# Query projections of five batches by Strassen's seven products, and the output projection begun one slot later

## The chip, the cores and the metric

The kernel runs on one core of one Trainium2 chip. The metric is the device time of one launch in microseconds (us); of several runs the median is given. A core has TensorE (PE, with its weight loads listed apart as PEld), VectorE (DVE), ScalarE (ACT), GpSimd (POOL) and SyncE (SP, which here only issues DMAs). Each engine works through its own list of instructions in the order in which the program wrote them and waits for semaphores of the others.

## The reference, cut to what matters

Cross-attention of 8 batches, 256 query tokens, 256 context tokens, width 1024, 32 heads of 32, all in fp32. The mask is all ones.

```python
x = (hidden - mu) * rsqrt(var + LN_EPS) * ln_gamma + ln_beta
Q = split_heads(x @ Wq.T)
scores = einsum('bhsd,bhtd->bhst', Q, K) * HEAD_DIM ** (-0.5)   # K, V: the context itself
probs = softmax(where(mask, scores, -inf))
attn = merge_heads(einsum('bhst,bhtd->bhsd', probs, V))
out = hidden + attn @ Wout.T
```

So each batch needs two products with a 1024 x 1024 matrix, 256 rows at a time: the query projection (Wq) and the output projection (Wout).

## The kernel before, in words

The program writes its own schedule. Its unit is a **slot** `n`, 0 to 63, of one group of four heads: `n = 8 * batch + group`. In slot `n` PE gets, in this order: the scores of group `n+1`; the product with V ("values") of group `n-2`; some steps of the output projection; one query tile (`make_q`, 8 matmuls of 256 columns, for a group six slots ahead); more steps of the output projection. Meanwhile the other engines run the softmax of group `n+1`. In the text, `i` is a slot's place in its batch, `n % 8`, and offsets are counted from the first scores matmul of the slot.

The softmax of a slot: DVE takes the mask and the maximum of eight 128x256 score tiles (L396), ACT takes their exponentials (L400) behind it, DVE the reciprocals of the sums (L407), POOL scales the eight tiles (L409, "normalize"), DVE transposes them in four 128x512 blocks (L415), ACT copies half of the blocks aside (L421), and SP issues the DMAs that bring the halves together (L472, L476), the loads of the slot between them.

Output projection (`product_steps`, L549). It is already made by Strassen's products: seven products `PRODUCTS` of four steps each, 28 steps for a batch, in the eight slots of the next batch. A step is one matmul of 512 columns whose weights are a block of the attention output `at` and whose moving operand is a block or a sum of blocks of Wout. The table `STEPS` says how many steps stand ahead of the query tile and how many behind the softmax's code in each slot. All accumulate in one PSUM bank, `po`, which has a single buffer: between certain products the bank is read out, by `keep` ("p1" on ACT, L559; "u2" and "u3" on DVE, L561) and `store` (DVE, L569, then a DMA by SP). Each read-out has to be done before PE's next step writes the bank. The sums of blocks of `at` are made by POOL (`sum_at`, L539): S1, S3, S2 at the end of slot `i = 1`, S4 in `i = 2`. Product S2 begins in slot `i = 2`, behind the query tile.

LayerNorm of later batches is spread over the slots: `bn_stats`, `bn_aggr` and `+eps` on DVE at the end of `i = 0` and `i = 1` (L211 to L216), and right behind them the power -1/2 on POOL (L217), which stands ahead of `sum_at` in POOL's list. The normalization is ACT's (L225, `i = 2, 3`), block transposes are DVE's (L290, `i = 3, 4`), and 16 small DMAs (`move_x`, L306) complete the transposed batch `xnT`.

`fold` multiplies Wq by gamma on POOL (L342) in slots 0 to 7 and copies the query bias to `qb` (L341). `sum_wo` (L177) makes the four Wout sums on POOL in slots 3 to 13.

The lines around the change, by their function in the listing: the query tile L319, its copy from PSUM to SBUF L327 to L333 on ACT, scores L362, values L492, copy of values to `at` L504.

## Time and profile before

| | us |
|---|---|
| median of 3 runs | 595.73 (595.67 to 596.32) |
| profiled execution, its own time | 596.43 |
| its span in the profile | 594.6 |
| PE busy | 582.0 |
| DVE / ACT / POOL busy | 458.3 / 407.0 / 347.5 |
| granted TensorE clock | 0.999 |

Times in the profile are counted from the span's start. `out<-in` are the program's names for tiles. A matmul of fp32 is kept as two records: the 56 query tiles of 8 matmuls with 256 columns are 896 records. In the list of groups a line ends with busy time, mean duration and the idle time ahead; in the timeline a line begins with start and length, merges equal neighbours, and ends with the idle time ahead of it and what ended it. A record's duration holds the pipeline's latency, so the cost of a matmul in a row of matmuls is the distance of starts, not the duration.

Slots are seen in the timeline by the first scores matmul: slot 33 (`i = 1` of a batch) begins at 305.70, slot 34 at 314.08, slot 35 at 323.35. In the steady part they last alternately 8.39 and 9.25 us, 70.56 for eight.

### The profile page before, as it was taken

How to read it: one execution, taken by the hardware profiler on the slowest of the kernel's cores; microseconds unless marked ns; L12 is line 12 of the kernel's file. 1: busy time of each engine (PE TensorE's matmuls, PEld its weight loads, DVE VectorE, ACT ScalarE, POOL GpSimd, SP SyncE). 2: the span in 40 equal slices, each digit the busy share in tenths (PEclk: the TensorE clock that was granted, in tenths of full speed). 3: DMA queues.
4: the chain of work that ended last, by engine and by line, in shares of the span. 5: the costliest groups of instructions: out<-in, count | busy, mean ns of one | idle time of the engine just before them, and what ended most of it. 6: DMA issues, size and time to landing. Idle time of an engine off the chain costs nothing.

```text
span 594.6 us, 18914 instructions
## 1 busy us (share of the span) xinstructions
PE 582.0 (98%) x6680; PEld 389.3 (65%) x6680; DVE 458.3 (77%) x1675; ACT 407.0 (68%) x1380; POOL 347.5 (58%) x630
## 2 busy tenths in 40 slices
PE   9999999999999999999999999999999999999997
PEld 8787776666666676666676667666666667654443
DVE  5878888697887878788787887878787677779801
ACT  4788786776777776686676876677677677667700
POOL 1568896987557644755447653484556564385600
PEclk9999999999999999999999999999999999999999
DMA  8566798545863667544674457654556355466541
GB/s 309 222 165 210 227 255 234 156 114 172 228 185 90 175 177 209 167 113 139 195 225 128 130 157 191 193 155 136 158 145 194 99 162 142 125 181 174 165 126 71
DMA packets 42063, 101.13 MB, mean 170 GB/s; under 512 B 8560, under 2 KB 8560, under 8 KB 41968
## 3 DMA queue, kind: packets, MB, share of 16 engines
q1 hardware_dynamic: 41680, 99.91, 57.4%
q8 instruction: 53, 0.87, 0.7%
q14 instruction: 42, 0.34, 0.2%
q10 hardware_dynamic: 288, 0.01, 0.0%
HBM read 51.65 MB, written 8.39 MB: 101 GB/s over the span
## 4 chain that ended last, share of the span: by engine, by line
PE 76%; POOL 12%; DVE 5%; issue 2%; DMA 2%; ACT 2%; SPq 1%; POOLq 0%; DVEq 0%; ACTq 0%
PE pq L319 29%; PE po_S L549 17%; PE sc L362 9%; PE pv L492 9%; POOL e L409 8%; PE po_A L549 7%; PE po L577 3%; DVE e L396 2%; POOL wo L177 2%; POOL wq L342 1%; PE busy L118 1%; DMA pT<-pc 1%; DVE pT L415 1%; DVE st L211 1%; DMA v<-in_kv_dram 1%
## 5 line engine op out<-in xcount | busy, mean ns | idle before, releaser
L409 POOL TENSOR_SCALAR e<-e,rden 128x256 f32<-128x256 f32 x512 | 237.3, 481 | 172.3 <-DVE rden L407 168.7
L400 ACT ACTIVATE e<-e,mn 128x256 f32<-128x256 f32 x512 | 254.3, 502 | 55.2 <-DVE mn L396 55.2
L319 PE MATMUL pq<-xnT,wq 128*128 128x256 f32 (+1 forms) x1008 | 230.7, 382 | 1.3 <-ACT q L327 1.2
L415 DVE STREAM_TRANSPOSE pT<-e 128x512 f32<-128x512 f32 x256 | 181.4, 709 | 55.4 <-POOL e L409 48.2
L319 PEld LDWEIGHTS pq<-xnT,wq 128*128 128x128 f32 x1008 | 188.9, 190 | 45.1 <-issue 17.9
L396 DVE CUSTOM_DVE_ANT_0 e<-sc,mb 128x256 f32<-128x256 f32 x512 | 185.4, 417 | 33.8 <-PE sc L362 33.5
L421 ACT COPY pc<-pT 128x512 f32<-128x512 f32 x128 | 79.2, 619 | 76.1 <-DVE pT L415 45.3
L549 PE MATMUL po_S<-wo,at 128*128 128x512 f32 x224 | 107.0, 603 | 3.3 <-DVE u L561 1.3
L400 ACT ACTIVATION_READ_ACCUMULATOR e<-e,mn 128x1 f32 x512 | 98.4, 192 | 0.0
L492 PE MATMUL pv<-pT,v 64*32 64x128 f32 x4096 | 74.6, 274 | 2.2 <-DMA pT<-pc 1.4
L362 PEld LDWEIGHTS sc<-k,q 32*128 32x128 f32 x1024 | 46.4, 184 | 46.3 <-issue 23.4
L362 PE MATMUL sc<-k,q 32*128 32x256 f32 x1024 | 74.3, 401 | 0.1
L492 PEld LDWEIGHTS pv<-pT,v 64*32 64x32 f32 x4096 | 57.3, 105 | 25.0 <-issue 12.9
L549 PEld LDWEIGHTS po_S<-wo,at 128*128 128x128 f32 x224 | 40.6, 189 | 38.8 <-issue 31.8
L549 PE MATMUL po_A<-wo,at 128*128 128x512 f32 x112 | 52.0, 598 | 0.0
L407 DVE RECIPROCAL rden<-den 128x2 f32<-128x2 f32 x256 | 39.3, 153 | 9.0 <-ACT e L400 6.3
L396 DVE DVE_READ_ACCUMULATOR2_ANT mn<- 128x1 f32 x512 | 42.7, 83 | 0.0
L549 PEld LDWEIGHTS po_A<-wo,at 128*128 128x128 f32 x112 | 20.8, 190 | 19.1 <-issue 18.4
L217 POOL TENSOR_TENSOR rstd<-ve,mhalf 128x1 f32<-128x1 f32 x16 | 9.4, 585 | 38.8 <-DVE ve L216 38.2
L504 ACT COPY at<-pv 128x128 f32<-128x128 f32 x128 | 26.1, 253 | 8.1 <-PE pv L492 8.1
L333 ACT ACTIVATE q<-pq,qb 128x256 f32<-128x256 f32 x48 | 22.6, 470 | 10.2 <-PE pq L319 10.2
L549 PE MATMUL po_S<-wo,s 128*128 128x512 f32 x56 | 26.9, 605 | 0.6 <-DVE r L569 0.6
(52 smaller groups left out, 299.7 us busy)
## 6 DMA issues: line engine op xcount, KB each, us to landing
v<-in_kv_dram SPq DMA_DIRECT2D x32, 512.0 KB, 4.3
pT<-pT SPq DMA_DIRECT2D x128, 128.0 KB, 2.3
pT<-pc SPq DMA_DIRECT2D x128, 128.0 KB, 3.9
k<-in_kv_dram SPq DMA_DIRECT2D x32, 256.0 KB, 3.4
x<-in_x_dram SPq DMA_DIRECT2D x14, 512.0 KB, 5.6
r<-in_x_dram SPq DMA_DIRECT2D x28, 256.0 KB, 4.4
out_dram<-r SPq DMA_DIRECT2D x28, 256.0 KB, 3.1
xnT<-xe SPq DMA_DIRECT2D x96, 64.0 KB, 3.1
```

Of the source, the lines that this page charges most:

```text
L319: nc.tensor.matmul(pqs[n], wq[:, o, c, :], xnTs[b](c), start=(c == 0), stop=(c == NC - 1),)
L333: nc.scalar.activation(q[:, :S].rearrange("p (s a k) -> p a s k", s=NS, a=NA), pqs.pop(n).rearrange("p (a s k) -> p a s k", s=NS, a=NA), A ...
L362: nc.tensor.matmul(scs[n][j][:, s, :], qs[n][r, ts(s, P)], ks[n - n % 2][r, n % 2, :], start=True, stop=True,)
L396: nc.vector.tensor_tensor_reduce(out=e[:, s, :], in0=pss[j][:, s, :], in1=mbs[n // NQ], scale=1.0, scalar=NO_SCORE, op0=ALU.add, op1=ALU.m ...
L400: nc.scalar.activation(e[:, s, :], e[:, s, :], AF.Exp, bias=mn[:, s : s + 1], scale=-1.0, accum_out=den[:, s : s + 1],)
L407: nc.vector.reciprocal(rden, dens[j])
L409: nc.gpsimd.tensor_scalar(es[j][:, s, :], es[j][:, s, :], rden[:, s : s + 1], 1.0, ALU.mult, ALU.mult,)
L415: nc.vector.transpose(pT[:, :, :, j, :, :].rearrange("p a i s k -> p (a i) s k"), es[j].rearrange("p s (b t) -> p b s t", t=K),)
L421: nc.scalar.copy(pc[:, :, ts(j, 2)], pT[:, 1, :, ts(j, 2)])
L492: nc.tensor.matmul(pvs[n][r][j * HD : (j + 1) * HD], vs[n - n % 2][ts(r, 2 * K), i, ds(n % 2 * P + j * HD, HD)], pT[ts(r, 2 * K), :, i, j, ...
L504: nc.scalar.copy(ats[b][:, c, :, ts(r, 2), :], pv.rearrange("p a s k -> p s a k"))
L549: nc.tensor.matmul(pos[b], operand(b, name)[:, c], wo[:, which, c], start=begins and c == 0, stop=c == NK - 1, skip_group_check=not begins,)
```

## The change

Queries of batches 3 to 7 are no longer made tile by tile, but as seven products of a Strassen scheme, one product in each slot of `i = 2, 3, 4, 5, 6, 7, 0`, none in `i = 1`. A product is 16 matmuls of 128 columns (`query_product`); its weights are 4 x 4 blocks of Wq or of sums of them, its moving operand is a quarter of `xnT` or a sum of quarters. Products accumulate in the `pq` bank; after each one `copy_product` reads it: four ACT activations for products 0, 1, 2, 5 and one DVE addition for 3, 4, 6. These copies stand behind the third transposed block in the softmax's code. The query of a batch lies in one tile `qa` with no second buffer, and its last column holds the bias, so that `qb` goes.

The sums of weights are made once on POOL (`sum_wq`, 16 additions of 128x512, in slots 9 to 20), the sums of quarters of `xnT` for each batch (`sum_x`, four additions: two in `i = 0`, one each in `i = 2` and `i = 3`). Three of the weight matrices, T1, B11 and T3, are written to DRAM once and come back through one tile `ring` of 1 MB, in two DMAs of 512 KB each, issued in `i = 0`, `i = 2` and `i = 4` of each batch, for the products of `i = 2`, `4` and `6`.

The output projection of batches 0 to 5 begins in `i = 1` in place of `i = 0`, has three places in a slot (behind the scores, behind the values, behind the softmax's code) and ends in `i = 0` of the batch after. Its first four steps stand in `i = 1` between scores and values, and `keep` "p1" is written right behind them, ahead of the softmax's code. Batch 6 keeps its former steps (`ENDS`). Query tiles of batches 0 to 2 go on as before, but slot 8 makes two and slot 9 none; the second of slot 8 uses the `po` bank.

Smaller parts: the mask is loaded batch by batch, 6 + 6 + 4 in place of 4 + 4 + 4 + 4 block moves in a slot, `at` in halves with three buffers, fewer buffers in `asp` and `sm`.

```diff
-    asp = ctx.enter_context(tc.tile_pool(name="asp", bufs=3))
+    asp = ctx.enter_context(tc.tile_pool(name="asp", bufs=2))
...
+    ring = const.tile([P, NK, NK, P], F32, tag="ring", name="ring")
+    sums_x = const.tile([P, 2, NK, NA, K], F32, tag="sx", name="sx")
+    kept = {
+        name: dram.tile([P, NK, NK * P], F32, tag=name, name=f"kept_{name}")
+        for name in ("T1", "B11", "T3")
+    }
...
     def fold(o):
 
-        nc.gpsimd.tensor_copy(qb[:, o : o + 1], qs[o][:, S:])
         nc.gpsimd.tensor_tensor(
-            wq[:, o], wq[:, o], gam.unsqueeze(2).to_broadcast([P, NC, P]), ALU.mult
+            wq[:, o], wq[:, o], gs.unsqueeze(2).to_broadcast([P, NC, P]), ALU.mult
         )
...
+    Q_PRODUCTS = (
+        ("S1", "ring", True), ("S4", "B22", False), ("A11", "ring", True), ("S2", "T2", False),
+        ("S3", "ring", False), ("A22", "T4", False), ("A12", "B21", True),
+    )
...
+    def query_product(b, p):
+        name, which, begins = Q_PRODUCTS[p]
+        if begins:
+            pqs[b] = ps_q.tile([P, NK, P], F32, tag="pq", name=f"pq_{b}_{name}")
+        x_ = x_part(b, name)
+        for o in range(NK):
+            w = weights(which, o)
+            for c in range(NK):
+                nc.tensor.matmul(
+                    pqs[b][:, o, :], w[:, c], x_[:, c], start=begins and o + c == 0,
+                    stop=c == NK - 1, skip_group_check=True,
+                )
...
-    STEPS = [((0, 4), (0, 3), (1, 3), (1, 2), (2, 2), (2, 1), (3, 1), (0, 3))] * (B - 2)
-    STEPS.append(((0, 4),) * 7 + ((0, 0),))
+    STEPS = ((0, 0, 0), (4, 0, 3), (0, 1, 2), (0, 2, 2), (0, 2, 1), (0, 1, 2), (0, 0, 3), (0, 1, 2),
+             (0, 2, 0))
+    ENDS = ((0, 0, 4),) * 7 + ((0, 0, 0),)
...
-    BATCH0 = (1, 2, 1, 1, 2, 1, 2, 1)
+    BATCH0 = (1, 2, 1, 1, 2, 1, 2, 1, 2, 0)
...
-                moves=tuple(first - 5 + i // 4 for i in range(16)),
+                moves=tuple(first - 5 + i // 6 for i in range(16)),
...
+    for n, which, *chunks in (
+        (9, "T1", 0, 1), (12, "T1", 2), (13, "T1", 3), (14, "T3", 0, 1), (15, "T3", 2, 3),
+        (16, "T2", 0, 1), (18, "T2", 2, 3), (19, "T4", 0, 1), (20, "T4", 2, 3),
+    ):
+        sums[n] += [partial(sum_wq, which, o) for o in chunks]
+    for n, b in firsts.items():
+        for slot, name in ((n - 2, "S1"), (n - 2, "S2"), (n, "S4"), (n + 1, "S3")):
+            sums[slot].append(partial(sum_x, b, name))
...
+    for n, b in firsts.items():
+        for slot, name in ((n - 2, "T1"), (n, "B11"), (n + 2, "T3")):
+            if b > SPLIT or name != "T1":
+                streams[slot] += [partial(load_ring, name, half) for half in range(2)]
...
         if n + 1 < N:
             scores(n + 1)
+        project_steps(n, 0)
+        hooks, now, behind = {}, [], []
+        for what, one, *args in evacuations[n]:
+            if what is keep and args == ["p1"] and one < B - 2:
+                keep(one, "p1")
+            elif one == B - 2:
+                now.append(partial(what, one, *args))
+            else:
+                hooks.setdefault(0 if i in (2, 3, 4, 6) else 1, []).append(partial(what, one, *args))
         if n >= 2:
             values(n - 2)
...
+        project_steps(n, 1)
+        copies = [partial(copy_q, q) for q in new_q[:1]]
         for q in new_q[:1]:
             make_q(q)
-
-        if b >= 0 and i == 1:
-            keep(b, "p1")
+        if n in products:
+            query_product(*products[n])
+            copies.append(partial(copy_product, *products[n]))
+        for one in now:
+            one()
...
-        if b >= 0:
-            product_steps(b, range(done, done + steps[i][1]))
-        for args in sums[n]:
-            sum_wo(*args)
+        project_steps(n, 2)
+        for one in sums[n]:
+            one()
         if b >= 0:
             for name in {1: ("S1", "S3", "S2"), 2: ("S4",)}.get(i, ()):
                 sum_at(b, name)
```

## The prediction

> **What bounds the kernel now.** First the page: busy times and the chain that ended last.

> ```profile
> PE 582.0 (98%) x6680; PEld 389.3 (65%) x6680; DVE 458.3 (77%) x1675; ACT 407.0 (68%) x1380; POOL 347.5 (58%) x630
> ...
> PE 76%; POOL 12%; DVE 5%; issue 2%; DMA 2%; ACT 2%; SPq 1%; POOLq 0%; DVEq 0%; ACTq 0%
> ```

> PE is the bound, and in the steady part it never waits: eight slots last 70.56 us, and that is the sum of their matmuls. POOL's 12% of the chain, listed in order of time, lies between 64 and 119 us (slots 5 to 12) and in the last five slots: early on POOL has no slack. What 128 columns cost is read from the timeline of PE: first the only query matmuls of that width (batch 0), then one slot with its query tile and three output steps.

> ```profile
> 12.52 2.05 PE L264 MATMUL pq<-xnT,wq 128*128 128x129 f32 x16
> 14.41 0.82 PE L319 MATMUL pq<-xnT,wq 128*128 128x257 f32 x3
> ...
> 305.70 1.15 PE L362 MATMUL sc<-k,q 32*128 32x256 f32 x16
> 306.77 1.16 PE L492 MATMUL pv<-pT,v 64*32 64x128 f32 x64
> 307.86 3.72 PE L319 MATMUL pq<-xnT,wq 128*128 128x256 f32 x16
> 311.42 2.74 PE L549 MATMUL po_A<-wo,at 128*128 128x512 f32 x6
> ```

> Starts count, not lengths: 16 records of 128 columns take 14.41 - 12.52 = 1.89, 16 of 256 take 311.42 - 307.86 = 3.56, 6 of 512 take 314.08 - 311.42 = 2.66. In each row one record costs 0.10 more (the first behind another kind, or the last before one), so a record costs 0.112, 0.216 and 0.429 us.

> Then the neighbours that the change leans on: slot 33 (`i = 1`) into slot 34, on ACT, POOL and PE.

> ```profile
> 305.81 0.59 ACT L559 COPY p<-po_A 128x512 f32<-128x512 f32 x1 [0.66 <-PE po_A L549]
> 307.39 0.51 ACT L400 ACTIVATE e<-e,mn 128x256 f32<-128x256 f32 x1 [1.00 <-DVE mn L396]
> ...
> 315.42 0.55 POOL L217 TENSOR_TENSOR rstd<-ve,mhalf 128x1 f32<-128x1 f32 x1 [2.43 <-DVE ve L216]
> 315.93 1.28 POOL L539 TENSOR_TENSOR s<-at 128x512 f32<-128x512 f32 x1
> 317.29 1.28 POOL L539 TENSOR_TENSOR at<-at 128x512 f32<-128x512 f32 x1
> 318.65 1.27 POOL L539 TENSOR_TENSOR at<-s,at 128x512 f32<-128x512 f32 x1
> ...
> 320.68 2.74 PE L549 MATMUL po_S<-wo,at 128*128 128x512 f32 x6
> ```

> The third sum ends at 319.92 and product S2, which needs it, starts at 320.68: 0.76 us of slack. Ahead of the sums POOL waits 2.43 for DVE's LayerNorm (`ve`), which stands behind the last transposed block, which needs the last exponential. So the sums follow ACT's first exponential (307.39) through four engines. In slot 10 this slack is already gone:

> ```profile
> 106.94 1.27 POOL L539 TENSOR_TENSOR at<-s,at 128x512 f32<-128x512 f32 x1
> ...
> 108.27 2.84 PE L549 MATMUL po_S<-wo,at 128*128 128x512 f32 x6 [1.00 <-POOL at L539]
> ```

> **The change, part by part.** The sum is made against the profiled execution's 596.4, which is 0.7 above the median.

> *Query matmuls.* 40 tiles of 3.56 = 142.4 go; 35 products of 0.10 + 32 x 0.112 = 3.69, 129.2, come: -13.2. The moving operand now has runs of 32 elements in place of 64; no row prices that, the quarter's row above (contiguous) is taken.

> [...] The 16 records above, each with its own full load, show 0.112, and the trace decides.

> *Mode changes.* In `i = 1` four steps stand between scores and values: one more 0.10 going in and one coming out, in slots 9, 17, 25, 33, 41, 49: +1.2. Slot `i = 1` then lasts 1.08 + 3.63 + 1.08 + 2.77 = 8.56.

> *The wait that comes.* `keep` "p1" (0.59 on ACT) stands ahead of the softmax's eight exponentials in ACT's list. Before, its product was finished when the slot began, at offset 0.11. Now it waits for the four steps: 1.08 + 0.10 + 8 x 0.429 = 4.61, the last record ends 0.16 later, so the copy runs to 5.4 and the first exponential moves from offset 1.69 to 5.4, +3.7. Queued behind: all exponentials (they run back to back at 0.49, nothing catches up), then reciprocals, normalizing, blocks, LayerNorm, POOL's power and three sums. These end at 319.92 - 305.70 + 3.7 = 17.9, that is 17.9 - 8.56 = 9.35 into `i = 2`. PE is at S2 at 6.60 + 0.13 (longer product) = 6.73. It waits 2.6. This holds in slots 26, 34 and 42: +7.8 (2.0 to 3.2 each: the slack and lags of the DVE are exact to some tenths). In slot 50 no LayerNorm is left; POOL ends normalizing at 7.29 + 3.7, the sums 3.9 later, at 6.3 of slot 50: no wait. In slot 18 PE comes late itself, as slot 17 still has a query tile: +0.2.

> *Slots 8 to 10.* Slot 8's second tile lies in `po`; ACT copies it at about 1.9 of slot 9 (its last aside copy there ends at 1.43, the copy takes 0.47) and the first step waits for that: +0.8. The exponentials then begin at 6.1 in place of 2.8; the POOL list of slot 9 gets two sums of weights (1.28 each, the rows of L177) ahead of the three sums. These end at some 11.9 of slot 10, and PE wants them at 6.6: 5.3, less the 1.0 that is there now: +4.3 (2 to 6).

> *Slots 11 to 20.* Fourteen more sums of weights stand in POOL's list. Working POOL's list through with 3.8 for normalizing and 1.28 a sum, normalizing begins 1 to 3 us late in slots 11 to 14, DVE's read-out of `po` in slots 14 and 15 comes 1.4 and 0.4 after PE wants the bank, and in slot 19 the second product waits 2.1 for its quarter's sum (two weight sums stand ahead of it); the 0.5 of waits now in slots 11 and 12 go: +3.4 (0 to 6).

> *The ring.* 15 reloads of 1 MB. SP is idle enough (it waits 155 us for ACT's copies alone); each issue costs it 0.5. Its T3 load follows the softmax's DMAs of `i = 4`, some 4.0 behind the last aside copy (in slot 32 from 305.14 to 309.14). With that slot's softmax 1 to 2 us late it starts near 6.0 of `i = 5`. Loads of this size land after 4.3 to 5.6:

> ```profile
> v<-in_kv_dram SPq DMA_DIRECT2D x32, 512.0 KB, 4.3
> ...
> x<-in_x_dram SPq DMA_DIRECT2D x14, 512.0 KB, 5.6
> ```

> So the first half is there at 1.8 to 3.1 of `i = 6`, and the product wants it at 2.26, the second half 1.8 later. 0.4 each, five times: +2.0 (0 to 2.5 each). T1 and B11 have half a slot more and are costed at nothing.

> *Copies.* ACT: sixteen activations of 128x128 (0.27, L268) a batch against eight of 0.47; behind the exponentials, covered as long as they end before the next product, half a slot later. DVE: three additions of 0.67 a batch. From its first maximum to its last block it needs 6.88 a slot, a read-out in between adds 0.47; with LayerNorm, mask and all that is 8 x 6.88 + 6 x 0.47 + 3 x 0.67 + 2 x 1.6 + 2 x 1.2 + 0.7 = 66 us a batch, against 70.56 - 8 x 3.56 + 7 x 3.69 + 0.2 = 68.1 of PE. Covered, but barely: a lag takes some four slots to die out. POOL's four `sum_x` lie in gaps, except where named.

> *The end.* In slots 59 to 62 DVE sets the pace (7.37 a slot, against 5.8 of PE's).

> ```profile
> 535.32 3.70 PE L549 MATMUL po_S<-wo,at 128*128 128x512 f32 x8 [0.64 <-DVE u L561]
> ```

> Slot 57 loses its query tile, but DVE follows only 1.6 earlier: 1.9 of the saving is not seen, +1.9.

> *The beginning.* `qb` goes (8 x 0.18 on POOL, which is on the chain there), the mask's 256 KB load shrinks: -1.0 (-2 to 0). Six block moves in a slot cost SP 1.2 there, with `xnT` wanted two slots later: nothing.

> Sum: -13.2 + 1.2 + 7.8 + 0.2 + 0.8 + 4.3 + 3.4 + 2.0 + 1.9 - 1.0 = +7.4, 603.8 by the profiled execution, 603.1 by the median; I say 603.

> **Rivals.** (a) *Nothing waits; faster.* The place that decides is S2 in `i = 2`: if the exponentials came less than 0.76 + 0.17 + 0.13 = 1.06 late, the sums would be there in time. Then only -13.2 + 1.2 + 1.9 - 1.0 = -11.1 is left: 585. For it: PE's 98%, and the wait is seen only in slot 10 before. Against it: the order in ACT's list, 3.7 late. (b) *POOL's early sums are absorbed*, as later slots give back the lag: without the 8.5 of slots 8 to 20, 594 to 598. Against it: slot 10's wait of 1.00 before. (c) *The ring is late.* If each T3 half lands as wq did in the start (9.5 us, busy DMAs), PE waits up to 2.5 more in `i = 6`, and DVE's lag grows with it: +11, 614. For it: DMA engines are 57% busy and get 16% more bytes. Against it: landings of 4.3 to 5.6 in the steady part.

> **How the numbers follow.** Forecast (599 to 610) 0.62; (a) 0.13; (b) 0.13, its sides 0.05 faster, 0.04 same, 0.04 slower; (c) 0.12. Range 592 to 613: it leaves out most of (a) and half of (c). A change under 0.2% can't be told from none. Faster 0.18, same 0.04, slower 0.78.

> **What would show it.** Product rows of 32 records, 3.6 us from start to start; in slots 26, 34, 42 "p1" at about 4.8, the first exponential at 5.4, and a wait of PE ahead of `po_S2` of 2.6 ended by POOL; a bigger one in slot 10; `i = 6` with a wait ended by the ring's DMA or none. Wrong if products run slower than 0.112 a record, if DVE falls behind for good, or if S2's wait is not there.

## The result, and the profile after

| | before | after |
|---|---|---|
| median of 4 runs, us | 595.84 (595.67 to 596.32) | 617.1 (616.2 to 619.02) |
| profiled execution, its own time | 596.43 | 617.79 |
| its span | 594.6 | 616.0 |
| PE busy | 582.0 (98%) | 579.7 (94%) |
| POOL busy | 347.5 | 391.0 |
| granted TensorE clock | 0.999 | 0.988 |

The change makes the kernel slower, by a ratio of 1.036 (95% interval 1.0332 to 1.0388). The prediction had 603 with a range to 613. The direction was right and the size was not: +7.4 was predicted and +21.4 came (span against span). So 14.0 us have to be found. They are sought in the profiled execution.

The page of after, its first part and the row of the granted clock (forty equal slices, tenths):

```profile
PE 579.7 (94%) x7160; PEld 395.9 (64%) x7160; DVE 461.6 (75%) x1690; ACT 411.4 (67%) x1420; POOL 391.0 (63%) x659
...
PEclk9999999899999999999999999999999999989999
```

PE does 2.3 us less and the span is 21.4 longer, so PE stands still for some 24 us more. The list of waits of after says for whom (engine, line, who ended the wait: total, times, longest):

```profile
PE po_S L659 <- POOL at L649: 18.2, 6, 5.0
PE po_A L659 <- ACT qa L339: 2.8, 1, 2.8
PE pq_S L430 <- POOL xnT L420: 1.5, 1, 1.5
```

Six waits for POOL's three sums make 18.2 of it: in slots 10, 18, 26, 34, 42 (all `i = 2`, as predicted) and 58 (the projection of batch 6, not predicted). The place predicted, slot 33 into slot 34, looks like this in the timelines of ACT, POOL and PE (start, length):

```profile
325.46 0.59 ACT L669 COPY p<-po_A 128x512 f32<-128x512 f32 x1 [2.74 <-PE po_A L659]
325.95 0.51 ACT L507 ACTIVATE e<-e,mn 128x256 f32<-128x256 f32 x1
```

```profile
323.75 0.55 POOL L229 TENSOR_TENSOR rstd<-ve,mhalf 128x1 f32<-128x1 f32 x1 [2.98 <-DVE ve L228]
324.87 1.27 POOL L420 TENSOR_TENSOR sx<-xnT 128x512 f32<-128x512 f32 x1 [0.57 <-DMA out_dram<-r]
326.21 1.27 POOL L420 TENSOR_TENSOR sx<-sx,xnT 128x512 f32<-128x512 f32 x1
327.46 0.94 POOL L516 TENSOR_SCALAR e<-e,rden 128x256 f32<-128x256 f32 x2
...
333.97 0.55 POOL L229 TENSOR_TENSOR rstd<-ve,mhalf 128x1 f32<-128x1 f32 x1 [2.43 <-DVE ve L228]
334.49 1.28 POOL L649 TENSOR_TENSOR s<-at,at 128x512 f32<-128x512 f32 x1
...
337.19 1.27 POOL L649 TENSOR_TENSOR at<-s,at 128x512 f32<-128x512 f32 x1
```

```profile
329.22 1.15 PE L469 MATMUL sc<-k,qa 32*128 32x256 f32 x16
...
332.34 3.73 PE L430 MATMUL pq_S<-sx,ring 128*128 128x128 f32 x32
338.51 3.56 PE L659 MATMUL po_S<-wo,at 128*128 128x512 f32 x4 [2.43 <-POOL at L649]
342.00 1.15 PE L469 MATMUL sc<-k,qa 32*128 32x256 f32 x16
```

Slot 33 begins at 320.65. The copy "p1" stands at offset 4.81, the first exponential at 5.30, the sums end 9.24 into slot 34 and PE waits 2.43. All of this is what the prediction had (4.8, 5.4, 9.35, 2.6). Two things it did not have. POOL's list in slot 33 holds two x sums (L420) ahead of normalizing, and normalizing (327.46) begins as they end. And the two output steps (four records) behind the wait last from 338.51 to 342.00, 3.49 us, where they take 1.91 behind the wait in slot 18, at a clock of 1.00, and 1.81 where PE does not wait (all three edits of order, below).

The second is the clock. The view by windows of after (stretch in us; its length; busy time of PE, PEld, DVE, ACT and POOL with the number of records; granted clock; DMA share; GB/s):

```profile
113.03:116.44 3.41, 0.01 (x1) 0.01 (x1) 0.00 (x0) 1.13 (x6) 3.25 (x4) 1.00 1.03 350
116.44:119.86 3.42, 3.42 (x4) 1.17 (x4) 2.23 (x5) 0.84 (x2) 3.42 (x8) 0.50 0.05 19
...
334.90:338.31 3.41, 1.18 (x11) 0.98 (x9) 2.47 (x15) 3.41 (x16) 3.25 (x3) 1.00 0.93 293
338.31:341.72 3.41, 3.21 (x4) 1.17 (x4) 2.01 (x5) 0.99 (x4) 3.41 (x9) 0.50 0.39 117
...
409.99:413.40 3.41, 1.42 (x4) 0.68 (x4) 1.37 (x5) 2.15 (x10) 3.33 (x6) 1.00 0.97 335
413.40:416.82 3.42, 3.42 (x42) 1.70 (x47) 2.80 (x9) 2.13 (x6) 3.42 (x7) 0.50 0.02 5
...
188.12:191.53 3.41, 1.73 (x16) 1.53 (x14) 3.41 (x19) 2.86 (x13) 3.06 (x3) 1.00 0.86 216
191.53:194.95 3.42, 2.09 (x8) 0.86 (x12) 1.24 (x5) 1.51 (x7) 3.41 (x6) 1.00 0.75 248
```

Behind the waits in slots 10, 34, 42 and 58 the clock is 0.50 for 3.41 us; the trace of before has no such stretch but at the very end (from 593.81 of 594.6 on). (Slot 58 is not shown: PE is busy for 0.62 of the 3.41 ahead of its stretch.) The wait of 3.01 in slot 18 (the last two lines) has none behind it. More on that below.

### The profile page after: what moved, and what is told of

Same layout as the page of the kernel before. It is cut to its first block, busy times and chain, and to the rows that moved or that the text cites. A ratio compares the mean times of both kernels' runs of the same rounds, so it can differ in the third digit from the quotient of the medians.

```text
span 616.0 us, 20038 instructions
## 1 busy us (share of the span) xinstructions
PE 579.7 (94%) x7160; PEld 395.9 (64%) x7160; DVE 461.6 (75%) x1690; ACT 411.4 (67%) x1420; POOL 391.0 (63%) x659
## 5 line engine op out<-in xcount | busy, mean ns | idle before, releaser
L659 PE MATMUL po_S<-wo,at 128*128 128x512 f32 x224 | 114.2, 632 | 18.9 <-POOL at L649 18.2
L330 PE MATMUL pq<-xnT,wq 128*128 128x256 f32 (+1 forms) x368 | 84.1, 382 | 1.2 <-ACT qa L337 1.2
L330 PEld LDWEIGHTS pq<-xnT,wq 128*128 128x128 f32 x368 | 68.7, 190 | 15.6 <-issue 3.9
L469 PEld LDWEIGHTS sc<-k,qa 32*128 32x128 f32 x1024 | 46.9, 186 | 44.6 <-issue 23.8
L469 PE MATMUL sc<-k,qa 32*128 32x256 f32 x1024 | 75.2, 405 | 0.1
L430 PEld LDWEIGHTS pq_A<-xnT,wq 128*128 128x128 f32 x320 | 37.3, 192 | 4.8 <-issue 4.5
L430 PE MATMUL pq_A<-xnT,wq 128*128 128x128 f32 x320 | 37.3, 275 | 0.0
## 6 DMA issues: line engine op xcount, KB each, us to landing
v<-in_kv_dram SPq DMA_DIRECT2D x32, 512.0 KB, 4.2
ring<-kept_T SPq DMA_DIRECT2D x18, 512.0 KB, 5.6
x<-in_x_dram SPq DMA_DIRECT2D x14, 512.0 KB, 5.1
```

The costliest lines, as they stand in the source:

```text
L330: nc.tensor.matmul(pqs[n], wq[:, o, c, :], xnTs[b](c), start=(c == 0), stop=(c == NC - 1),)
L430: nc.tensor.matmul(pqs[b][:, o, :], w[:, c], x_[:, c], start=begins and o + c == 0, stop=c == NK - 1, skip_group_check=True,)
L469: nc.tensor.matmul(scs[n][j][:, s, :], qa[r, n % NQ, ts(s, P)], ks[n - n % 2][r, n % 2, :], start=True, stop=True,)
L659: nc.tensor.matmul(pos[b], operand(b, name)[:, c], wo[:, which, c], start=begins and c == 0, stop=c == NK - 1, skip_group_check=not begins,)
```

## The experiments

Below, a slot's length is counted from its first scores matmul to the next slot's. Without any wait the eight slots `i = 0` to `7` last 7.65, 8.56, 8.51, 9.37 and four times 8.51 (so they stand in the runs below), 68.13 against 70.56 before. A difference to before "at slot n" is counted from the start of slot 0.

### The later output projection alone

All queries in tiles; no products, no sums of weights or x, no ring.

```diff
-    SPLIT = 3
+    SPLIT = B
...
-        (9, "T1", 0, 1), (12, "T1", 2), (13, "T1", 3), (14, "T3", 0, 1), (15, "T3", 2, 3),
-        (16, "T2", 0, 1), (18, "T2", 2, 3), (19, "T4", 0, 1), (20, "T4", 2, 3),
...
-        (9, "B11", 0), (10, "B11", 1), (12, "T1", 0), (14, "T1", 1), (15, "T3", 0), (16, "T3", 1),
```

> The later output projection alone: the changed kernel with all 64 query tiles made tile by tile (no products, no sums of query weights, no ring). Theory A: a slot i = 1 holds a query tile as well and lasts 12.0, so the late sums are there in time at S2 in i = 2 (17.9 - 12.0 = 5.9 against 6.6); what stays is 1.2 of mode changes, the start of slot 9 that waits for ACT (3 to 4) and a wait of 2 to 3 in slot 10: 603, 600 to 606, with no stretch of low clock. Rival D (the later projection itself costs the time, by the copy ahead of the softmax, with or without products): 595.8 + 21 + 11 = 628, since the products' saving is missing too.

Measured: 601.69 (601.44 to 602.44), ratio 1.01 (1.0083 to 1.0117), as expected. The clock is 1.00 in the whole of it. At the end of slot 10 it is 3.9 us behind the kernel before (1.99 of waiting in slot 9 for ACT's copy of the second tile, 2.56 for the sums in slot 10), at the end 5.2. So the later projection costs some 5 to 6, nearly all of it at the two ends, and in the steady part 0.2 for each batch (70.73 against 70.56). The other 15 us come with the products, which by themselves save 2.6 a batch.

### The copy "p1" behind the exponentials

```diff
-                keep(one, "p1")
+                hooks.setdefault(2, []).append(partial(keep, one, "p1"))
...
             exps(2)
+            for hook in hooks.get(2, ()):
+                hook()
             normalize(0)
```

> One edit to the changed kernel: the copy "p1" of batches 0 to 5 is written behind the sixth exponential in ACT's list in place of ahead of the first. Theory A (the copy waits for four output steps and holds up the softmax, hence POOL's sums; PE's wait for them also lowers its clock): the three sums end near 14.2 + 0.6 - 8.56 = 6.3 of slots 26, 34 and 42, ahead of PE's 6.7, so the waits there (1.6, 2.4, 3.0) and the low clock behind those of slots 34 and 42 are gone; slot 10's wait falls from 5.0 to 1 to 2 with no low clock; slot 18 stays. 617.1 - 17 = 600, 597 to 604. Rival B (POOL simply has too much work, 391 us against 347, whatever the order in ACT's list): the sums stay late, 613 or more.

Measured: 619.82 (616.96 to 622.49), ratio 1.0399 (1.0357 to 1.0441). A miss of 20 us. In the trace the wait for S2 is gone, and a bigger one stands in the slot before, for "p1" itself. PE in slots 33 and 34 of this run:

```profile
327.16 4.54 PE L661 MATMUL po_A<-wo,at 128*128 128x512 f32 x6 [2.96 <-ACT p L671]
...
334.75 3.73 PE L430 MATMUL pq_S<-sx,ring 128*128 128x128 f32 x32
338.32 1.88 PE L661 MATMUL po_S<-wo,at 128*128 128x512 f32 x4
```

The three steps (six records) behind the values write the only `po` bank, which "p1" gives back. I had counted only what the copy holds up on ACT, not who waits for the copy. Slots 25 to 26 last 13.06 + 8.68 in place of 8.57 + 11.22 in after. It is no test of whether the exponentials' delay reaches S2, as slot 33 is now so long that everything is in time.

### LayerNorm's power behind the three sums

```diff
-        nc.gpsimd.tensor_tensor(rstds[b][:, s : s + 1], ve, mhalf[:, :1], ALU.pow)
...
             for name in {1: ("S1", "S3", "S2"), 2: ("S4",)}.get(i, ()):
                 sum_at(b, name)
+            if i == 1:
+                for args in stats[n]:
+                    ln_power(*args)
```

> One edit to the changed kernel: in i = 1 POOL's power -1/2 for LayerNorm stands behind the three sums for S2 in place of ahead of them; the copy "p1" stays where it is. Theory A (the chain runs late exponentials, normalizing, then LayerNorm's DVE work, the power, the sums): without LayerNorm in it the sums start when normalizing ends, 10.9 of i = 1, and end near 6.3 of i = 2, as they do in slot 50: no wait in slots 26, 34, 42, some 12 us less, plus 2 to 3 in slot 10; 602, 599 to 607. Rival B (POOL's amount of work): 613 or more.

Measured: 606.32 (602.39 to 607.97), ratio 1.0164 (1.0125 to 1.0202), 11 us better than after. The sums no longer stand behind DVE's LayerNorm. What was late next in slots 33 and 34 of this run, on POOL, on DVE and on PE:

```profile
320.50 1.28 POOL L427 TENSOR_TENSOR sx<-xnT 128x512 f32<-128x512 f32 x1 [2.46 <-DMA pT<-pT]
...
323.10 3.67 POOL L523 TENSOR_SCALAR e<-e,rden 128x256 f32<-128x256 f32 x8
```

```profile
331.85 0.69 DVE L686 TENSOR_TENSOR r<-po_A,r 128x512 f32<-128x512 f32 x1
```

```profile
332.68 1.95 PE L666 MATMUL po_S<-wo,at 128*128 128x512 f32 x4 [1.94 <-DVE rden L521]
```

The sums end at 330.7, but PE starts at 332.68, right behind DVE's read-out of the bank (`store`, 331.85 + 0.69). DVE comes to it late, because its blocks wait for normalizing, and normalizing begins only when the x sums are through, at 323.10, 8.7 into slot 33. The longest wait of PE in slot 34 falls to 1.94, and the two steps behind it take 1.88 (332.68 to 334.56), for 3.49 in after; behind none of the waits in slots 26, 34 and 42 does the clock halve.

### Six exponentials ahead of "p1"

```diff
+                hooks[2] = [partial(keep, one, "p1")]
...
+            late = hooks.get(2, ())
+            if late:
+                exps(1)
+                exps(2)
+                for hook in late:
+                    hook()
             for done in list(pvs):
                 copy_at(done)
```

> Edit: in the slots i = 1 ACT's list has six of the softmax's exponentials ahead of the copy p1, the copy of the attention values behind it, then the last two exponentials. So the copy still runs at 4.8 to 5.4 and gives the bank back before PE wants it at 5.8 (in the run with the copy behind all of the exponentials PE waited 3.0 for this bank). If the place of that copy in ACT's list is alone what makes S2's sums late, the last exponential ends 2.3 earlier in slots 25, 33 and 41, the three sums end at about 7.0 of the next slot, the waits there are 0.3 at most and the half-clock stretches there go: 617.1 - 11.4 - 2.5 (slots 9 and 10) = 603 (600 to 607). Rival: two sums of x (S1 and S2 of the next batch's products, 2.6 us) stand on POOL ahead of the normalizing in i = 1 and run from 3.9 to 6.6, so that normalizing can't begin before 6.6 whatever ACT does; the sums then end at about 8.8 in place of 9.25, the waits stay at 1.2 to 2.6, and only slots 9 and 10 gain: 612 (609 to 616). The trace of after, in which the x sums end at 6.56 and normalizing begins at 6.68, makes me take the rival as the likelier.

Measured: 612.07 (610.57 to 614.46), ratio 1.0274 (1.0248 to 1.03): the rival's 612. POOL in slots 33 and 34 of this run (slot 33 begins at 317.1, slot 34 at 326.91):

```profile
321.29 1.28 POOL L420 TENSOR_TENSOR sx<-xnT 128x512 f32<-128x512 f32 x1 [0.53 <-DMA out_dram<-r]
...
323.89 3.66 POOL L516 TENSOR_SCALAR e<-e,rden 128x256 f32<-128x256 f32 x8
329.98 0.55 POOL L229 TENSOR_TENSOR rstd<-ve,mhalf 128x1 f32<-128x1 f32 x1 [2.43 <-DVE ve L228]
```

Six exponentials are done by 323.5, and still normalizing starts at 323.89, behind the x sums. The three sums end 17.4 behind the start of slot 33, where they end 17.8 behind it in after. So the copy's place in ACT's list is not alone what makes them late; the x sums hold POOL's list to nearly the same point. The copy came at 6.4 of the slot, not 4.8, since DVE's maxima are late, and PE waits 1.17 for the bank in `i = 1`.

### All three: exponentials first, x sums one slot later, power behind

The two edits above, and

```diff
-        for slot, name in ((n - 2, "S1"), (n - 2, "S2"), (n, "S4"), (n + 1, "S3")):
+        for slot, name in ((n - 1, "S1"), (n - 1, "S2"), (n, "S4"), (n + 1, "S3")):
```

> Edit: the six exponentials ahead of p1, and besides it the two x sums one slot later and LayerNorm's power behind the three sums, so that POOL's order in i = 1 is normalizing, x sums, the three sums, power. The slots 8 to 21 keep their schedule. If S2's wait in i = 2 is the sum of these three delays on the way from the exponentials to the sums, it is gone: normalizing ends near 8.3 of i = 1, the x sums near 2.4 of i = 2 (the product wants them at 3.1), the sums near 6.3, S2 wants them at 6.7. Slots 26, 34, 42 of 8.5 to 8.8, 43 of 9.4, no half-clock stretch but in slot 58 (and 10, if its wait stays at 3 or more): -11.4; slot 18 -2.4, slots 9 and 10 -3: 600 (597 to 604). Rival (PE then waits for something else in the same slots, such as the x sums ahead of the product): 606 to 612.

Measured: 601.35 (600.64 to 602.33), ratio 1.0092 (1.0077 to 1.0107). PE in slots 33 and 34 of this run:

```profile
319.04 2.84 PE L673 MATMUL po_A<-wo,at 128*128 128x512 f32 x6 [1.17 <-ACT p L683]
...
324.94 3.73 PE L437 MATMUL pq_S<-sx,ring 128*128 128x128 f32 x32
328.51 1.88 PE L673 MATMUL po_S<-wo,at 128*128 128x512 f32 x4
```

Neither the product nor S2 waits; slots 26, 34 and 42 last 8.51, 8.51 and 8.57 in place of 11.22, 12.79 and 12.65. 1.17 is paid for the bank in `i = 1`. Slot 19, in the early part that kept its schedule, gets longer: 13.28 for 11.15 in after, by a wait of 2.02 for an x sum with a half-clock stretch behind it.

### The same with "p1" put back ahead of all exponentials

```diff
-                hooks[2] = [partial(keep, one, "p1")]
+                keep(one, "p1")
```

> Edit: the run with the six exponentials ahead of p1, the x sums one slot later and the power behind the three sums (601.35), with p1 put back ahead of all exponentials. POOL's order stays the mended one. If p1's place is one of the delays on the way to the sums, normalizing ends again near 2.3 of i = 2 in place of 8.3 of i = 1, the x sums near 4.9 and the three sums near 8.9: the product waits 1.5 to 2 for its x sum and S2 some 0.3 behind it, slots 26, 34 and 42 last 10.3 to 10.9 and the slots 25, 33 and 41 before them 8.6; together 19.2 against 18.3 in that run: 601.35 + 3 x 0.9 + 1 = 605 (602 to 609). Rival (POOL's order alone makes the wait, p1's place nothing): slots 26, 34 and 42 at 8.5, and, with 25, 33 and 41 at 8.6 for 9.8: 598 (596 to 600).

Measured: 610.38 (609.02 to 614.99), ratio 1.027 (1.0225 to 1.0315). POOL and PE in slot 34 of this run, which begins at 322.21:

```profile
324.49 1.26 POOL L427 TENSOR_TENSOR sx<-xnT 128x512 f32<-128x512 f32 x1
325.83 1.27 POOL L427 TENSOR_TENSOR sx<-sx,xnT 128x512 f32<-128x512 f32 x1
327.06 1.28 POOL L656 TENSOR_TENSOR s<-at,at 128x512 f32<-128x512 f32 x1
...
329.78 1.27 POOL L656 TENSOR_TENSOR at<-s,at 128x512 f32<-128x512 f32 x1
```

```profile
325.95 3.81 PE L437 MATMUL pq_S<-sx,ring 128*128 128x128 f32 x32 [0.45 <-DMA ring<-kept_T]
331.10 1.98 PE L666 MATMUL po_S<-wo,at 128*128 128x512 f32 x4 [1.34 <-POOL at L656]
```

The x sums begin at 2.3 of slot 34 and the sums end at 8.8, as expected (2.3, 8.9); slots 26, 34 and 42 last 10.8 (10.3 to 10.9 expected). The waits are split otherwise than expected: in slot 34 the product waits 0.45 and S2 1.34, and in slot 42 it is T1's load that is waited for (1.56) and S2 hardly (0.20), so that there the number fits by luck. So "p1" ahead of the exponentials is one of the delays, and POOL's order is the other: mending one alone leaves a wait. The whole is 5 above my number, through a wait in slot 50 (10.79 for 8.63), one in slot 10 (11.49 for 8.51) and a half-clock stretch in slot 58, none of which I had counted.

### Useless matmuls ahead of the wait

Half of the first product is computed twice in `i = 2` (the result is overwritten), and the query tile of slot 10 likewise.

```diff
-        for o in range(NK):
+        for again in ((2, NK) if p == 0 else (NK,)):
+            for o in range(again):
```

> The changed kernel with useless work for PE ahead of its waits for S2: the first half of product 0 is computed twice (32 records become 48, 1.8 us more) in slots 18, 26, 34, 42 and 50, and the query tile of slot 10 twice (3.5 us more). Theory A2 (three of the four stretches of 3.4 us at half clock follow from PE's idle time ahead of S2): PE idles less than 2 us there, the stretches in slots 10, 34 and 42 are not there, only that of slot 58; 3 x 1.7 = 5.1 less, and 2.0 more for the work that no wait covers (slots 26 and 50): 614. Rival C (the slow output steps behind the waits come from contention, the clock follows from them or is not the cause): they stay slow, and the time is 617 + 2 = 619 or more.

Measured: 617.9 (615.61 to 623.6), ratio 1.0382 (1.0328 to 1.0436), not to be told from after. The clock stayed at 1.00 through slots 10 to 57 (by windows: 1.00 from 329.10 to 342.80). PE in slot 34 of this run:

```profile
333.60 5.60 PE L431 MATMUL pq_S<-sx,ring 128*128 128x128 f32 x48 [1.48 <-DMA ring<-kept_T]
339.63 1.98 PE L660 MATMUL po_S<-wo,at 128*128 128x512 f32 x4 [0.43 <-POOL at L650]
```

The two steps last 1.98 in place of 3.56. But the product itself came 1.5 late, for T1, and the sums ended at 10.7 of the slot in place of 9.24, because the x sums came 1.9 later in the slot before (6.1 for 4.2). And slot 6, which has a half-clock stretch in this run, lasts 13.51 for 10.16 in after. So what the clock had taken was lost elsewhere. The run speaks for PE's idling as the cause of the half clock; its time alone would have shown nothing.

### Slots 8 to 21 with another schedule

The sums of weights start in slot 11 and end in 21, T1 and T3 go to DRAM later, the second query tile goes from slot 8 to slot 9, x sums stand ahead of the sums of weights.

```diff
-    BATCH0 = (1, 2, 1, 1, 2, 1, 2, 1, 2, 0)
+    BATCH0 = (1, 2, 1, 1, 2, 1, 2, 1)
...
-        (9, "T1", 0, 1), (12, "T1", 2), (13, "T1", 3), (14, "T3", 0, 1), (15, "T3", 2, 3),
-        (16, "T2", 0, 1), (18, "T2", 2, 3), (19, "T4", 0, 1), (20, "T4", 2, 3),
+        (11, "T1", 0), (12, "T1", 1), (13, "T1", 2), (14, "T1", 3), (15, "T3", 0, 1),
+        (16, "T3", 2, 3), (18, "T2", 0, 1), (19, "T2", 2, 3), (20, "T4", 0, 1), (21, "T4", 2, 3),
```

> Edit: only the schedule of slots 8 to 21 is moved. The sums of weights start in slot 11 in place of 9 and end in 21; T1 and T3 go to DRAM one or two slots later; slot 8's second query tile goes to slot 9; x sums stand ahead of the sums of weights. The steady part is left as it is. If POOL's list in slots 9, 10, 17 and 19 and the late copy of the second tile make the early loss: slot 9 without its wait of 2.8, slot 10's wait 5.0 down to 2.5 or less and no half clock there (-4 to -6), slot 18's wait of 3.0 down to 0.5 (-2.5), slot 19's wait for the x sum of 1.5 gone (-1.5), against up to +2 of new waits in slots 11 to 16 and 20: 617.1 - 11 + 1 = 607 (603 to 611). Rival (the work is only moved, and POOL or DVE give the same lag some slots later): 613 to 618, with the same difference at slot 21 as in after, 14.5.

Measured: 609.19 (607.64 to 610.88), ratio 1.0223 (1.0199 to 1.0248). The difference to before at the end of slot 21 is +4.8 in place of +14.5. The gain is made in slots 8 to 10, which last 26.87 for 37.01, and in slot 19, 9.37 for 11.15: in after the first step of slot 9 waits 2.82 for ACT's copy of slot 8's second tile, here it does not wait, and slot 10's wait falls from 5.00 to 0.36. In slot 17 of after POOL's next sum of weights waits for the DMA that takes T3 to DRAM, with everything of that slot behind it:

```profile
177.17 2.51 POOL L381 TENSOR_TENSOR wq<-wq 128x512 f32<-128x512 f32 x2 [3.60 <-DMA kept_T<-wq]
...
182.22 3.67 POOL L516 TENSOR_SCALAR e<-e,rden 128x256 f32<-128x256 f32 x8
```

Slot 18, where the prediction had 0.2, lasts 12.40 for 8.51 there. But in this run, where no sum of weights waits for that DMA in slot 17, slot 18 stays at 12.21, so my number for it was wrong. POOL and PE of this run, slots 17 and 18:

```profile
168.82 1.27 POOL L420 TENSOR_TENSOR sx<-xnT 128x512 f32<-128x512 f32 x1 [3.46 <-DMA kept_T<-ring]
```

```profile
184.49 1.98 PE L659 MATMUL po_S<-wo,at 128*128 128x512 f32 x4 [3.00 <-POOL at L649]
```

POOL now waits as long for a DMA ahead of its first x sum, and PE waits 3.00 for S2 as before (3.01). In the run with the three edits of order and the old schedule POOL waits even 4.11 for T3's DMA, and PE only 1.14; with both mended (below) it does not wait. So T3's DMA alone does not make slot 18 late; the order of `i = 1` is needed for it.

### Both orders mended

The moved schedule of slots 8 to 21 and the three edits of order together.

> Edit: the order of the run before on ACT and POOL together with the moved schedule of slots 8 to 21. If both losses are separate, they add: 600 - 8 = 592 (588 to 597), with the difference to the kernel before at slot 21 not above +5, and falling by 2.4 for each batch behind it. Rival (the early lag comes from DVE and POOL being full, not from the order): 598 to 604.

Measured: 596.45 (592.74 to 600.42, 10 runs), ratio 1.0013 (0.9991 to 1.0036), 4 above my 592, in its range. At slot 21 the difference to before is +1.7; slots 18, 26, 34 and 42 last 8.51. The gains of the two edits alone, 15.8 and 7.9, would make 23.7 if they added; 20.7 was measured, so they are separate in the main (slot 10's wait goes in either, but for 0.36). What is left: the bank in `i = 1` (3.5), slot 58 (3.2 and a half-clock stretch), T3, and 3 to 4 in slot 6 (below).

### Without the ring

The ring is loaded 14 times in after, not 15 (28 halves in its list of DMAs): batch 3's T1 is still in the buffer. The query projection of batches 3 to 7 is not the reference's here: T1, B11 and T3 are not loaded again.

```diff
-                streams[slot] += [partial(load_ring, name, half) for half in range(2)]
+                pass
```

> Edit: the changed kernel without the fifteen reloads (each in two halves) of T1, B11 and T3 from DRAM; all five batches then use in three of their products what lies in the buffer, T1, so the query projection is not the reference's. All waits for the ring go, and 15 MB of traffic. If the ring costs only its own waits (the profile of after: 0.6, 1.6, 0.0 and 0.6 in slots 22, 30, 38 and 46, 0.8 in slot 26): 617.1 - 3.6 = 613.5 (611 to 616). Rival (c of the prediction, the ring is late and makes lags behind it): 606 to 610.

Measured: 616.84 (613.98 to 617.36), ratio 1.0344 (1.0319 to 1.0368); the profiled execution has a span of 612.2. All slots `i = 6` last 8.51, and slots 26, 34 and 42 11.20, 12.75 and 11.74. The ring costs its own waits and no more; rival (c) of the prediction, a lag of 11 made by the ring, falls. The other runs lie 3 higher than the profiled one, so a price is not to be read from the median. The waits are not T3's alone: for T1, which the prediction costed at nothing, PE waits 0.75 in slot 26 of after, and up to 1.86 in other versions (slot 26 of the moved schedule).

### T3's loads ahead of the softmax's DMAs

```diff
+        if n - 2 in firsts:
+            for stream in streams.pop(n):
+                stream()
+            streams[n] = []
         if n + 1 < N:
             softmax(n + 1, copies, between, hooks, fill)
```

> Edit: to the kernel of the run before that had everything, one more: in the slots i = 4 the two reloads of T3 are issued on SP ahead of the softmax's DMAs and not behind them. There the loads started at 7.1 of i = 5 and landed 5.5 later, and the product waited for them 2.4 in slot 30 and 0.9 in slot 38. If SP's order makes that wait, the loads start at about 7.7 of i = 4, when the product that reads the buffer ends, and no slot i = 6 waits: 596.45 - 3.3 = 593 (590 to 596; each run has its own number of half-clock stretches, 1.7 us each). Rival (the load or the softmax's own DMAs then come late and the wait goes elsewhere): 596 to 600.

Measured: 593.74 (589.32 to 597.92, 10 runs), ratio 0.996 (0.9932 to 0.9989): the one version that is faster than before, by 0.4%. SP's loads and PE's product of slot 30, first in the run without this edit, then in this one:

```profile
277.72 1.02 SPq L404 DMA_DIRECT2D ring<-kept_T  x2
```

```profile
283.69 3.81 PE L437 MATMUL pq_A<-sx,ring 128*128 128x128 f32 x32 [2.35 <-POOL e L523]
```

```profile
268.30 1.01 SPq L404 DMA_DIRECT2D ring<-kept_T  x2
```

```profile
280.33 3.84 PE L437 MATMUL pq_A<-sx,ring 128*128 128x128 f32 x32
```

Issued 8.5 us earlier against the slot (9.87 ahead of slot 30, for 1.39), the loads are there in time; all slots `i = 6` last 8.51. But slot 42 lasts 10.80 in this run, for 8.51: there PE waits twice for T1 (0.95 and 0.83). The times of the two versions overlap, so the gain of this edit is shown by slots 30 and 38 and not by the medians. In the first pair the wait is put down to POOL, which had long been done; 277.72 and a landing of 5.5 say that it was the DMA.

### Two more edits

To the run before: "p1" behind four exponentials, and in slot 57 the three sums right behind the copy of the values.

```diff
             if late:
                 exps(1)
-                exps(2)
                 for hook in late:
                     hook()
...
+        early = n == N - NQ + 1
+        if early:
+            hooks[3] = [partial(sum_at, b, name) for name in ("S1", "S3", "S2")]
```

> Edit: the run before with two more: p1 behind four of the exponentials in place of six (PE waited 1.17 for its bank in slots 25, 33 and 41), and in slot 57 the three sums ahead of the normalizing in POOL's list (PE waited 3.24 for S2 in slot 58, and a half-clock stretch followed). 593 - 3 x 1.1 - 3.2 - 1.7 + 1.5 (the normalizing that is now behind the sums delays DVE, which sets the pace at the end) = 586 (583 to 590), faster than the kernel before by 1.2 to 2.1%. Rival (the end is DVE's: what PE does not wait for in slot 58 it waits for in 59 to 62, and the four exponentials end too late for S2): 590 to 594.

Measured: 595.22 (592.25 to 600.81, 10 runs), ratio 1.0003 (0.9973 to 1.0032): the rival. Slots 25, 33 and 41 gain 1.0 each and slots 26, 34 and 42 are 1.2, 0.7 and 0.9 longer than 8.51 (waits for T1 of 0.86 and 0.67 in slots 26 and 42, for S2 of 0.44 in slot 34). In slot 58 POOL's sums are early, and PE waits 4.22 in place of 3.24, now for DVE's read-out of the bank, which stands behind blocks that wait for the later normalizing.

## Why the prediction was right or wrong

**Query matmuls and mode changes: right.** Eight slots without waits last 68.13 against 70.56, and 70.73 with the later projection alone: 2.6 a batch, 13.1 in five (predicted -13.2), and +0.2 a batch for the mode (predicted +1.2 in six). The rows of 32 records stand at 3.6 to 3.7.

**S2 in slots 26, 34 and 42: place and size right, the mechanism only half.** PE's waits are 1.46, 2.43 and 3.05 against 2.6 each; with the product's own lateness (0.75 for T1 in slot 26) and without the clock the three slots lose 8.9, against 7.8 (+1.1). But the step "queued behind: all exponentials, then reciprocals, normalizing" named one of two chains that end together: in slot 33 the reciprocal that normalizing needs is there at 327.2, and the x sums, which I had put "in gaps", end at 327.5. That did not change the sum. It is why another place for "p1" alone (612) cured only a part; the first try at it (620) failed because I had not counted who waits for "p1" itself.

**The step that failed most: every wait was priced at its length.** In slots 10, 34, 42 and 58 the work behind the wait runs at half clock: 3.60 for two steps in slot 10 and 3.49 in slot 34, in place of 1.81 (the run with all three edits); 5.1 for four in slot 58 in place of 3.6. With 1.7 (half of 3.41) for slots 42 and 43 that is 6.7 us. No row of before could show it, as its PE nowhere idled that long in one stretch (1.35 at most).

**Slots 8 to 20: total too small, terms wrong.** Slot 9's wait is 2.8 for 0.8: the copy of the second tile comes at 3.4, not 1.9, since it stands behind another copy aside that waits for DVE (+2.0). Slot 10's is 5.0 for 5.3. "Slot 18 +0.2" measured 3.9 (+3.7). Its reason, that PE comes late itself, did not hold: PE waits 3.01 there. Two things hold the sums up, T3's way to DRAM, a DMA that I had not set against POOL's list at all, and the order of `i = 1`; without the first slot 18 lasts 12.21, with the order mended 9.91, with both 8.51. Slots 14 and 15, 1.8 predicted, have no wait (-1.8); slot 19 1.8 for 2.1.

**Ring.** Slots 22, 30, 38 and 46 lose 2.8, for 2.0 (+0.8). **The beginning** gave nothing for -1.0 (+1.1). **The end**: slots 57 to 61 last 36.9 for 37.1, although a tile of 3.56 is gone from them; of the 3.3 that are not seen, 1.5 is the stretch counted above, which leaves 1.8 for the predicted 1.9.

6.7 + 1.1 + 2.0 + 3.7 - 1.8 + 0.8 + 1.1 = 13.6 of the 14.0. Smaller pieces are left: slot 8 lasts 1.0 longer than before, slot 50 0.4 longer than without waits, and slots 10 and 19 wait 0.3 less each than predicted. They make 0.8, so the account closes to 0.4.

**The rivals.** (a), nothing waits, 585: the version with all orders mended and the early T3 comes to 593.7, and still waits for the bank, for T1 in slot 42, in slot 58 and at half clock. (b), the early losses are absorbed: wrong, the +14.3 at the end of slot 20 is +14.9 at the end of slot 33, and no slot between is shorter than its length without waits; where the losses were taken away (the moved schedule), they stayed away. (c) fell, though its 614 is the nearest number: that it came so near was luck.

## What to carry to other kernels

A copy that is moved ahead of an engine's queue, and an operation added to one, has two sides: who queues behind it and who waits for it. Where two chains end within tenths of a microsecond of each other, taking away one cures only a part (in slots 25, 26, 33, 34 and 41 to 43, where all edits of order together gain 8.5 us, "p1" behind six exponentials alone gains 2.6 and the power alone 4.1); the trace of the mended kernel has to be read for the next in line. On a kernel whose PE is 98% busy, price a new wait of 2 to 3 us or more with what follows it too: in after some 1.7 us more at a clock of 0.50 (3.49 for 1.81 in slot 34) behind four of the six waits of 2 us or more, from 80 us on to 20 us before the end, which depends on where the wait falls.

## What the runs showed of the hardware that I had not expected

```profile
323.79:327.20 3.41, 0.45 (x30) 0.18 (x16) 1.30 (x7) 2.96 (x12) 3.33 (x6) 1.00 0.93 290
327.20:330.62 3.42, 3.42 (x4) 1.44 (x5) 2.77 (x6) 2.03 (x6) 1.92 (x5) 0.50 0.67 229
395.47:398.88 3.41, 1.57 (x66) 0.89 (x64) 1.70 (x12) 2.05 (x10) 3.00 (x4) 1.00 0.90 263
398.88:402.29 3.41, 2.29 (x6) 1.06 (x6) 2.40 (x6) 2.68 (x10) 3.23 (x8) 1.00 0.87 260
```

In slot 33 the wait lies in one cell (PE busy 0.45 of 3.41), and the slot lasts 13.29; in slot 41 it is cut by the grid (1.57 and 2.29 busy), and the slot lasts 11.59. The difference, 1.70, is half of 3.41. In the run without the ring the clock is 0.50 for two such lengths behind slot 10's wait, from 113.96 to 120.79, though PE is busy for 2.64 of the first 3.41. This also bears on why runs of one of these kernels lie several us apart (589 to 598 for the fastest), where those of before agree within 0.8: in the ten runs of the fastest the mean granted clock goes from 0.999 (span 587.5) down to 0.988 (596.1), nearly in the order of their times. In the version without T3's edit it follows them less well (0.996 at a span of 590.9, 0.997 at 594.0), so this is not the whole of it.

**Open.** Some of the experiments' profiles have a half-clock stretch in slot 6, before 80 us, and neither before nor after has it. In the run with useless matmuls the slot lasts 13.51 for 10.16 with it. In the run with the power behind the three sums the clock is 0.51 from 69.20 to 72.60 and 0.50 from there to 76.00, behind 3.40 us in which PE is busy for 2.70 by the records (3.38 in after, clock 1.00). The 16 records of the scores that begin in them last 2.47 from the first start to the last end, where they take 1.15 in the steady part, and 1.32 of waiting for a query copy follows, so the busy share may be too high, but that was not tested.
